# Who issues the loads that bring chunks of edge records back from DRAM: SyncE instead of GpSimd

## The chip, the cores and the metric

The kernel runs on one core of one Trainium2 chip. A core has engines with queues of their own: TensorE (PE in the profile; its weight loads are PEld), VectorE (DVE), ScalarE (ACT), GpSimd (POOL) and SyncE (SP). SyncE computes nothing: it issues DMA transfers. Each engine takes its instructions strictly in the order in which they stand, and an instruction that waits holds up all that stand behind it on its engine. The metric is device microseconds (us) of one execution.

## What is computed

The reference is one layer of a graph network, followed by a mixture of experts; what matters here is its edge part:

```
x  : 3125 nodes x 512        src, dst : 50000 edges, sorted by the dst that was drawn
out = segment_sum(edge_feat(x[src], x[dst], edge_attr), edge_dst)   # edge_dst = src array
x   = x + gnn(layernorm(x)) + linear_attention(layernorm(x))
x   = x + moe(layernorm(x))                                          # 8 experts, 2 per node
```

Every edge needs a record (its attributes through a small softplus layer, the two node numbers, a place). The sums go to the node that the edge points at, so the kernel first sorts the records by that node, in DRAM.

## The kernel before

It has three stages, one after the other.

**Stage 1** makes the records, sorts them and does all work by nodes. The 392 tiles of 128 edges are 14 chunks of CT = 28 tiles. For chunk c, `records(c)` (line 239) computes places (`at_i`, lines 210 to 232, VectorE) and records (`rec`), and stores them with one transfer of 672 KB, in the order of arrival, to the DRAM tensor `lined` (line 273, SyncE). `recall(c)` (line 382) brings such a chunk back to SBUF, to the tile `again`, of which there are two. `place` (line 387) then writes the chunk's 28 tiles one by one to their places in the DRAM tensor `recs`, with an indirect DMA each (line 395, GpSimd): 392 scatters. A chunk can be recalled when its store has landed, and when all 28 scatters of the chunk two before it have landed, since they read the buffer that it takes.

The node work beside it comes in three parts. `layer_norm(t)` (line 327) runs for 25 tiles of 128 nodes: it loads x (line 333, SyncE), normalizes, stores a first share of the output (line 353, SyncE), transposes, and ends with matmuls into `ps_kx` (line 364). Then come the products of the query features for 7 groups of nodes and 2 halves (line 535, `ps_nm`). Last, for 25 tiles again, the rows that the edges will gather are computed: the last matmul of a tile is line 620, the result lies in a tile `r` of which there are two (lines 600, 608, 609), and SyncE stores it to `rows_d` and `rows_s` (lines 610, 611), loads y (line 554) and stores y (line 626). A tile's `r` can be written again when both stores of the tile two before it have landed.

Some scatters are held back on purpose: `place(upto, behind)` hangs the first scatter of a group on a matmul ("POOL gives way to PE"), one on each of the 25 layer norms, on each of the 14 query products and on each of tiles 0 to 23 of the last part. A scheduler with costs of its own sets the order on every engine in stage 1. It puts a scatter that is held back behind others that are not, so the last scatter of a chunk stands on GpSimd among those of the next.

**Stage 2** (`run_pairs`, line 905) is written out by hand: SyncE fetches sorted records (line 699), GpSimd gathers rows (lines 710, 714), and 212 pairs of tiles pass through all engines. The first fetch waits for all 392 scatters. **Stage 3** (`run`, line 1242) is the mixture of experts.

Of the kernel before, what the change touches and what calls it, by code (L numbers as in the profile page):

```python
# [43 lines left out]
def gnn_mix_moe_kernel(ctx: ExitStack, tc: tile.TileContext, a: dict, out: bass.AP):  # L44
# [5 lines left out]
    nc = tc.nc  # L50
# [41 lines left out]
    lined = dram.tile([T // CT, P, CT, REC], F32, name="lined")  # L92
# [30 lines left out]
    with ExitStack() as c1:  # L123
# [256 lines left out]
        again = {}  # L380

        def recall(c):
            if c < T // CT:
                again[c] = chk.tile([P, CT, REC], F32, name="again", bufs=2)
                nc.gpsimd.dma_start(again[c], lined[c])

        def place(upto, behind=None):

            for t in range(len(placed), min(T, max(0, int(upto / 1.3)))):
                c, i = divmod(t, CT)  # L390
                if t == 0:
                    recall(0)
                if i == CT // 2:
                    recall(c + 1)
                put = nc.gpsimd.indirect_dma_start(  # L395
                    out=recs[:, :], out_offset=bass.IndirectOffsetOnAxis(ap=at_i[:, t : t + 1], axis=0),
                    in_=again[c][:, i, :], in_offset=None,
                )
                if behind is not None:
                    tc.add_manual_dep(  # L400
                        put.ins, behind.ins.name,
                        mybir.DependencyInfo(mybir.DependencyClass.Sync, mybir.DependencyReason.DATA),
                        reason="POOL gives way to PE",
                    )
                    behind = None
                placed.append(put)
# [998 lines left out]
```

## Time and profile before

| | |
|---|---|
| three runs | 2907.07, 2907.54 (median), 2909.65 us |
| the profiled execution | 2907.43 us, of which the span from first to last instruction 2905.7 us |
| mean granted TensorE clock | 0.942 |
| busy: PE, DVE, ACT, POOL | 86%, 64%, 50%, 61% |
| transfers of `lined` and `again` | 14 of 672 KB each |
| stage 1 | 0 to 658.6 us (the first fetch of stage 2) |

The profile's page gives busy time by engine, a picture of the span in 40 slices (72.6 us each), the DMA queues, the chain that ended last, and the costliest groups of instructions. The trace behind it can be asked for one tile's instructions, or for all instructions of a stretch in order of time; such a line has the start, the duration, the engine, the line of the code, the operation with output and input, the number of merged instructions and, in brackets, how long the engine was idle before and what ended it. SPq and POOLq are the sequencers that issue transfers.

### The profile page before, as it was taken

The page shows a single profiled execution, that of the slowest core. Times are in us where ns is not written, and L with a number is a line of the kernel's source. Part 1 is how long each engine was busy: PE and PEld are TensorE (multiplying, and loading weights), DVE is VectorE, ACT ScalarE, POOL GpSimd, SP SyncE. Part 2 cuts the span into 40 slices and gives each one's busy share as a digit, 9 for nine tenths or more (in the row PEclk, how much of TensorE's full clock was granted, in tenths as well). Part 3 has the DMA queues.
Part 4 walks back from the last instruction along what each step waited for, and adds up shares of the span by engine and source line. Part 5 has one row for each costly group of instructions (what it writes and reads, how often), then busy time and mean ns, then how long its engine had stood idle before and what let it go on. Part 6 is the DMA issues. An engine that isn't in the chain of part 4 may idle for free. (4 is left out here: it accounts for less than half of the span.)

```text
span 2905.7 us, 41979 instructions
## 1 busy us (share of the span) xinstructions
PE 2508.4 (86%) x13530; PEld 1631.8 (56%) x13530; DVE 1865.2 (64%) x3864; ACT 1463.4 (50%) x4183; POOL 1762.2 (61%) x1756
## 2 busy tenths in 40 slices
PE   2685999005999999999999999997499999999998
PEld 2463466003444444444444444444388888888887
DVE  5887322005999999999999999996722222222222
ACT  2472422003888888888888888884311111111111
POOL 1777766677766666666666666750255555555553
PEclk8897999556999999999999999999799999999999
DMA  6662066107888888888888887853642622975452
GB/s 261 205 221 86 27 234 217 44 27 236 268 258 258 259 257 258 255 262 257 258 258 257 259 258 251 256 181 116 252 150 72 226 87 71 323 276 200 168 189 98
DMA packets 191644, 588.10 MB, mean 202 GB/s; under 512 B 54405, under 2 KB 79418, under 8 KB 179384
## 3 DMA queue, kind: packets, MB, share of 16 engines
q0 software_dynamic: 135216, 496.50, 52.4%
q1 hardware_dynamic: 49864, 82.54, 8.5%
q10 hardware_dynamic: 6336, 6.28, 0.7%
q8 instruction: 111, 1.82, 0.2%
q14 instruction: 117, 0.96, 0.1%
HBM read 635.54 MB, written 119.53 MB: 260 GB/s over the span
## 5 line engine op out<-in xcount | busy, mean ns | idle before, releaser
L884 PE MATMUL ps_s<-ft,one 128*128 128x512 f32 x1696 | 765.3, 594 | 2.1 <-DVE ft L871 2.0
L710 POOL DMA_INDIRECT gd<-rows_d,rec x424 | 429.7, 1013 | 266.0 <-DVE h L758 158.2
L714 POOL DMA_INDIRECT gx<-rows_s,rec x424 | 434.9, 1026 | 129.2 <-issue 123.4
L395 POOL DMA_INDIRECT recs<-again,at_i x392 | 413.7, 1055 | 156.2 <-issue 122.1
L867 ACT ACTIVATE ft<-ft,rec 128x128 f32<-128x128 f32 x1272 | 395.3, 389 | 193.8 <-DVE ft L860 193.7
L884 PEld LDWEIGHTS ps_s<-ft,one 128*128 128x128 f32 x1696 | 312.2, 194 | 310.7 <-issue 231.2
L1280 ACT ACTIVATE h<-ps_f,bias 128x128 f32<-128x128 f32 x318 | 116.7, 367 | 620.8 <-PE ps_f L1267 617.0
L1267 PE MATMUL ps_f<-h,we 128*128 128x128 f32 x3392 | 401.3, 277 | 0.0
L1282 DVE TENSOR_SCALAR h<-ps_f,bias 128x128 f32<-128x128 f32 x318 | 111.4, 351 | 433.4 <-PE ps_f L1267 429.4
L1267 PEld LDWEIGHTS ps_f<-h,we 128*128 128x128 f32 x3392 | 386.9, 192 | 1.4
L1194 POOL DMA_INDIRECT we<-w_rows,w_at x212 | 215.1, 1014 | 222.2 <-PE ps_y L1298 98.0
L734 PE MATMUL ps_ip<-ident,prod 128*128 128x128 f32 x1272 | 165.9, 281 | 172.1 <-DVE prod L726 172.1
L734 PEld LDWEIGHTS ps_ip<-ident,prod 128*128 128x128 f32 x1272 | 140.3, 143 | 252.1 <-issue 249.3
L822 ACT ACTIVATE dot<-gx,rec 128x128 f32<-128x128 f32 x848 | 270.6, 397 | 0.0
L812 DVE TENSOR_TENSOR wt<-wt,wb 128x1024 f32<-128x1024 f32 x212 | 257.7, 1216 | 0.0
L805 PE MATMUL wb<-w_s,hT 32*128 32x512 f32 x848 | 240.8, 644 | 2.9 <-DVE wt L812 2.9
L801 PE MATMUL wa<-w_f,hT 32*128 32x512 f32 x848 | 240.0, 642 | 0.0
L726 DVE TENSOR_TENSOR prod<-gd,gx 128x768 f32<-128x768 f32 x212 | 201.9, 952 | 23.1 <-DMA gx<-rows_s,rec 23.1
L1267 PEld LDWEIGHTS ps_f<-xt,we 128*128 128x128 f32 x1696 | 199.4, 193 | 26.0 <-issue 23.4
L871 DVE TENSOR_TENSOR ft<-gx,wt 128x768 f32<-128x768 f32 x212 | 205.7, 970 | 0.0
L1267 PE MATMUL ps_f<-xt,we 128*128 128x128 f32 x1696 | 199.8, 277 | 0.7 <-ACT xt L1215 0.7
L1298 PE MATMUL ps_y<-we,h 128*128 128x512 f32 x424 | 196.1, 605 | 0.0
(303 smaller groups left out, 3755.6 us busy)
## 6 DMA issues: line engine op xcount, KB each, us to landing
w_rows<-in_Wh POOLq DMA_DIRECT2D x24, 1024.0 KB
rows_s<-r SPq DMA_DIRECT2D x24, 448.0 KB
recs<-zero POOLq DMA_DIRECT2D x10, 1056.0 KB
rec<-recs SPq DMA_DIRECT2D x106, 96.0 KB
lined<-rec SPq DMA_DIRECT2D x14, 672.0 KB
again<-lined POOLq DMA_DIRECT2D x14, 672.0 KB
w_rows<-in_Wo POOLq DMA_DIRECT2D x8, 1024.0 KB
gd<-rows_d,rec POOLq DMA_INDIRECT x424
```

The lines of the kernel that those rows point to most:

```text
L395: put = nc.gpsimd.indirect_dma_start(out=recs[:, :], out_offset=bass.IndirectOffsetOnAxis(ap=at_i[:, t : t + 1], axis=0), in_=again[c][:, ...
L710: nc.gpsimd.indirect_dma_start(out=Q.gd[:, (i + 2) % G, :], out_offset=None, in_=rows_d[:, :], in_offset=bass.IndirectOffsetOnAxis(ap=reci ...
L714: Q.last = nc.gpsimd.indirect_dma_start(out=Q.gx[:, i, :], out_offset=None, in_=rows_s[:, :], in_offset=bass.IndirectOffsetOnAxis(ap=reci[ ...
L734: nc.tensor.matmul(ps[:, i, :], Q.prod[:, i, b * P : (b + 1) * P], ident, is_transpose=True, start=(b == 0), stop=(b == 2),)
L801: nc.tensor.matmul(wa[:, k, :], Q.hT[r, 0, :], w_f2[r, :], start=True, stop=True)
L805: nc.tensor.matmul(wb[:, k, :], Q.hT[r, 1, :], w_s2[r, :], start=True, stop=True)
L812: nc.vector.tensor_mul(R.wt, R.wt, wb)
L822: nc.scalar.activation(R.dot[:, c - 1, k, :], x[:, i, c * MUL : (c + 1) * MUL], AF.Copy, scale=Q.rec[:, i, c : c + 1])
L867: nc.scalar.activation(R.ft[:, k, D + c * MUL : D + (c + 1) * MUL], R.ft[:, k, 2 * D :], AF.Copy, scale=Q.rec[:, i, c : c + 1],)
L884: nc.tensor.matmul(R.ps, R.one[:, k, :], R.ft[:, k, m * D : (m + 1) * D], start=(k == 0 and m == 0), stop=(k == 1 and m == 1),)
L1194: nc.gpsimd.indirect_dma_start(out=dst, out_offset=None, in_=src, in_offset=bass.IndirectOffsetOnAxis(ap=at[:, j : j + 1], axis=0), bounds ...
L1267: nc.tensor.matmul(pss[f], ws[l][:, k, f * P : (f + 1) * P], h[:, k, :], start=(k == 0), stop=(k == 3))
```

## The change

The transfer that brings a chunk back is issued by SyncE instead of GpSimd:

```diff
         def recall(c):
             if c < T // CT:
                 again[c] = chk.tile([P, CT, REC], F32, name="again", bufs=2)
-                nc.gpsimd.dma_start(again[c], lined[c])
+                nc.sync.dma_start(again[c], lined[c])
```

Bytes, buffers and what waits for what stay the same; the waits of the 14 transfers now stand in SyncE's queue, between its loads and stores. The scheduler also orders stage 1 anew: on PE, DVE and ACT the lines of `records`, `layer_norm` and `by_random` change places among each other, on GpSimd some scatters do. Stages 2 and 3 keep their order.

## The prediction

> **What bounds the kernel now.** I read first the page's picture in 40 slices, for the stage that the change touches, then the answer for the tile `again`, then instructions in order of time on POOL, SP and PE.
>
> ```profile
> PE   2685999005999999999999999997499999999998
> POOL 1777766677766666666666666750255555555553
> ```
>
> Slices 8 and 9 (508 to 653 us): PE has nothing to do, POOL works on. Stage 1 ends with the scatters.
>
> ```profile
> L395 POOL DMA_INDIRECT recs<-again,at_i x392: 952/958/14968, 67.3 to 656.3; - x196
> L385 POOL DMA_DIRECT2D again<-lined x14: 542/579/593, 52.9 to 612.3; - x14
>   DVE acc L684: 149.5, 1
> ```
>
> In the rows the durations are min/median/max in ns. Scatters are issued from 67.3 to 656.3 us, and the first write of stage 2's sums (L684) waits 149.5 us. PE's last matmul of stage 1 ends at 510.8, so the node work had about 146 us to spare against the scatters' end.
>
> What a scatter and a recall cost POOL is seen late in the stage:
>
> ```profile
> 568.03 0.96 POOL L395 DMA_INDIRECT recs<-again,at_i  x1 [0.30 <-issue]
> 570.46 0.58 POOL L385 DMA_DIRECT2D again<-lined  x1 [1.47 <-DMA recs<-again,at_i]
> 575.39 0.98 POOL L395 DMA_INDIRECT recs<-again,at_i  x1 [4.35 <-DMA again<-lined]
> 576.68 0.95 POOL L395 DMA_INDIRECT recs<-again,at_i  x1 [0.31 <-issue]
> ```
>
> A scatter takes 0.96 + 0.30 = 1.26 us. The recall waits 1.47 us until the scatter before it has landed, and the scatter behind it starts 4.93 us after the recall's start, when the chunk has landed. Nearly every recall is such a turn: the two buffers and the held-back scatters make the chain (last scatter of a chunk, landing, recall, landing, next chunk). Its length does not hang on who issues.
>
> **The change, part by part.** I count scatters by their place on POOL, from 0, and recalls by their chunk. The order of the built programs gives, for both, which scatter is the last of chunk c-2 and which the first of chunk c.
>
> *What goes from POOL.* Recall 2 stood between free scatters:
>
> ```profile
> 126.47 0.96 POOL L395 DMA_INDIRECT recs<-again,at_i  x1 [0.30 <-issue]
> 127.43 0.58 POOL L385 DMA_DIRECT2D again<-lined  x1
> 128.32 1.16 POOL L395 DMA_INDIRECT recs<-again,at_i  x1 [0.30 <-issue]
> ```
>
> 128.32 - 126.47 is 1.85, less 1.26: 0.6 us gained, and 0.6 again at recall 3. Recall 4 cost 209.43 - 205.57 - 1.26 = 2.6.
>
> *The turns.* New length, from the start of a chunk's last scatter to the first that reads the recalled chunk: 0.96 + 1.47 to the landing, then 0.3 (SP's transfers show 0.3 to 0.6 on its sequencer) and 4.5 to the recall's landing, sum 7.2 us. No transfer of this size with free engines is seen on SP. Bounds: 3.1 (96 KB, issued on SP at 658.63, gather at 661.69) and 9.2 (`lined` of chunk 1, issued at 53.18 beside weight loads; the wait ended at 62.39). I take POOL's row, 4.93, as the same bytes move. Each us more or less here is 1 us per turn. Before, the turns took, for recalls 5 to 13: 8.2, 7.8, 9.1, 9.5, 8.3, 10.8, 7.9, 7.4, 10.2. Against 7.2 they shorten by 1.0, 0.6, 1.9, 2.3, 1.1, 3.6, 0.7, 0.2 and 3.0 us. Recall 4 is a new turn: in the new order the last scatter of chunk 2 stands straight before the first of chunk 4 (before, ten were between): 7.2 - 1.3 = 5.9 lost. Running sum: 0.6 + 0.6 + 2.6 - 5.9 = -2.1 after recall 4; +9.1 before recall 12; +12.3 at the end. POOL alone would start its last scatter at 656.3 - 12.3 = 644.0.
>
> *What comes to SP.* Recalls 3 to 13 stand in its queue ahead of loads and stores, and wait for POOL. SP is free again at "start before, less the running sum, plus 2.7" (0.96 + 1.47 + 0.3). One scatter of 14.97 us (at 251.7, beside VectorE's L450 to L452, straight after the layer norms) moves with these, so I leave out 14 us from there to recall 7. SP is free of recalls 3 to 13 at 148, 220, 265, 307, 365, 404, 440, 483, 522, 562, 603.
>
> Behind recall 3 stand the x loads of layer norms 7 and 8:
>
> ```profile
> 118.58 0.33 SPq L273 DMA_DIRECT2D lined<-rec  x1
> 119.00 0.38 SPq L333 DMA_DIRECT2D x<-in_x  x1
> ```
>
> 119.0 becomes 149. Recall 4 holds layer norms 13 to 16, recall 5 norms 17 to 22, recall 6 the last two: x at 311 instead of 221.5. Norm 17 ended 20 us after its x was issued, norm 24 (253) 31 us after; so the last one now ends at 331 to 342, the first `ps_nm` (300) comes 47 us later at 378 to 389, tiles 0 and 1 (364) another 64 later at 442 to 453. All this, and the new order on PE, DVE and ACT, is hidden by the 146 us above. The issue itself, 14 times 0.33 us, is nothing on SP, which mostly waits.
>
> Then SP stands at recalls 7 to 10 until 483, and only then stores tiles 0 and 1; tiles 2 and 3 need their `r`. Behind recall 11 stand the stores of tiles 4 to 7, behind recall 12 (562) those of 8 to 14, behind recall 13 (603) from 15. So the spare time is used up, and the last leg is from recall 12 on. Its pattern is in the trace: two tiles' stores, then two more tiles, then the next group:
>
> ```profile
> 367.02 0.32 SPq L611 DMA_DIRECT2D rows_s<-r  x1
> ...
> 372.95 0.51 ACT L600 COPY r<-ps_p 128x416 f32<-128x416 f32 x1 [4.17 <-DMA rows_s<-r]
> ```
>
> Tile 0's `rows_s` (367.02) lets tile 2's copy start 5.9 us later, and tile 4's last matmul ends at 389.05: 22.0. With 1.2 from SP's release to `rows_s` of tile 8, tile 12 ends at 562 + 23 = 585. From tile 12 (440.04) to tile 24 (510.79) 70.8 us pass: 656. Recall 13 delays only the store of tile 15, which tile 17 needs 10 us later. The first fetch stands behind tile 24's stores on SP, the last issued 0.8 us after the last matmul; with one landing (2.5) it comes at 657 to 659. Before it came at 658.6.
>
> *PE's clock.* The granted clock was 0.50 from 260 to 280, while PE stood nearly idle, 0.55 from 280 to 285 and 1.00 after. In the new waits PE falls idle for 10 us and more, and pays such a start, at most 2.5 us (5 at half speed), on the last leg once: I take 1.5. The Trainium skill (TensorE: Matmul & The Clock Gate, Part 1) puts the warm-up at about 3.4 us at half clock; by that it would be 1.7.
>
> **The sum.** First fetch at 658 + 1.5 to 660, against 658.6: +0.5. Each release sends a burst (recall, two tiles' stores, a y: 2.3 MB, 9 us at the 261 GB/s seen from 365 to 402); a recall (364.75) was under way in the pattern's 5.9 us too, so I add only 1. Stages 2 and 3 keep their order and shift as a whole. 2907.4 + 1.5 is **2909 us**; the profiled execution is 0.1 below the median, so nothing is corrected. Own range 2901 to 2917: 4 from nine turns at 0.5, 4 from the leg.
>
> The Trainium skill (DMA: Bandwidth & Descriptors, Issuing engines are not separate DMA queues) says that all issuers share the same transfer engines and another issuer saves only its time to issue. By that alone 14 recalls at 0.6 us save 8. But the same page (Anatomy of one DMA) says that a wait is kept on the issuing sequencer: that speaks against the change, and here SP has most behind it.
>
> **The rivals.** I call 0.2% (5.8 us) about what a measurement can tell from no change.
>
> 1. *POOL stays the bound, and wins.* If the node work ends before 644, the fetch comes at 644.0 + 2.3 = 646.3: -12.3, or **2895 us**; with turns that gain only half of that, 2901. For it: 2 of the 22 us of the pattern were spent on matmuls which PE can do during the wait. Against it: 70.8 us of matmuls behind tile 12, at a clock already at 1.00. It decides from recall 12 at 549 or earlier, or a shorter leg.
>
> 2. *The ring of waits bites: slower.* POOL waits for SP's recall, SP for POOL's scatter, and scatters hang on matmuls whose x or `r` lie behind SP. Scatter 219 (401 us) hangs on the first `ps_nm` (378 to 389): 12 us to spare or more; scatter 330 (559) on tile 7, by the same pattern (tile 3's last matmul ended at 376.7) at 522 + 1.2 + 9.7 = 533: 26; scatter 358 (600) on tile 12 (585): 15. If the tiles behind a release take 10 us longer than the pattern, the last leg is 10 longer: 2919. From 15 on the scatters wait too: with 25, scatter 358 is 10 late, and the leg makes it **2934**; with more, recall 12 itself comes late, and the excess counts twice, up to 2950. For it: bursts, cold PE, a scheduler that does not know POOL's real pace. Against it: the pattern's row already holds a burst.
>
> 3. *Nothing moves*: the scheduler's order alone, with recalls harmless. 2907; only if SP never waits, which the order of 7 to 10 in a row excludes.
>
> **Chances.** Forecast 0.56 (faster 0.08, same 0.33, slower 0.15); rival 1 0.18, nearly all faster; rival 2 0.24, slower; rival 3 0.02. Together: faster 0.25, same 0.36, slower 0.39. The range leaves out little below and 0.1 of rival 2, from its own point on: 2895 to 2934.
>
> **What would show it.** No L385 on POOL, 14 on SPq; SP idle at L385 for 29 us before recall 3 and longer at recalls 8 to 10; layer norm 24 at 331 to 342; PE with short gaps up to 656 instead of empty slices 8 and 9; last scatter at 644 to 653, held by L620. Wrong it is if PE's last matmul of stage 1 comes before 645 (rival 1), or scatters wait for L364, L535 or L620 for 10 us and more before recall 12 (rival 2).

## The result, and the profile after

The changed kernel takes 2921.5 us (median of five, 2918.3 to 2927.2) against 2907.6 for the kernel before (median of five): ratio 1.0049, 95% interval 1.0033 to 1.0064, so 14 us slower. The forecast was 2909 and the range 2895 to 2934: the range holds it, "no change" does not. The profiled execution took 2926.8 us with a span of 2925.0, 5.3 us above the median, and all places in time below are from it.

The picture in slices and the answer for the tile `again`, after:

```profile
PE   2545595693999999999999999997589999999998
POOL 1776766665766666666766666650255555555553
```

```profile
L395 POOL DMA_INDIRECT recs<-again,at_i x392: 952/958/14626, 68.0 to 653.8; - x196
L385 SPq DMA_DIRECT2D again<-lined x14: 319/326/339, 52.1 to 607.7; - x14
...
  DMA again<-lined: 48.9, 9
  PE ps_own L620: 5.0, 3
```

PE's empty slices 8 and 9 are gone, PE works up to the end of stage 1, and scatters wait for the landing of a recall (48.9 us, 9 times) and, at the end, for L620. GpSimd is done 2.6 us earlier than before. But the first fetch of stage 2 comes not at 658.6 but at 673.4. The end of stage 1 before, with GpSimd's last scatter, SP's first fetch and GpSimd's first gather:

```profile
656.32 0.96 POOL L395 DMA_INDIRECT recs<-again,at_i  x1 [0.30 <-issue]
661.69 0.99 POOL L710 DMA_INDIRECT gd<-rows_d,rec  x1 [4.41 <-DMA rec<-recs]
```

```profile
658.63 1.76 SPq L699 DMA_DIRECT2D rec<-recs  x4
```

The same after, with PE's last matmul and SP's queue:

```profile
653.76 0.95 POOL L395 DMA_INDIRECT recs<-again,at_i  x1 [3.44 <-PE ps_own L620]
678.99 0.99 POOL L710 DMA_INDIRECT gd<-rows_d,rec  x1 [24.28 <-DMA rec<-recs]
```

```profile
659.45 0.60 PE L620 MATMUL ps_own<-w_ndo,xg 128*53 128x128 f32 x4
```

```profile
659.34 0.24 SPq L610 DMA_DIRECT2D rows_d<-r  x1
660.52 0.23 SPq L611 DMA_DIRECT2D rows_s<-r  x1
660.84 0.44 SPq L626 DMA_DIRECT2D out<-y  x1
673.37 5.47 SPq L699 DMA_DIRECT2D rec<-recs  x6
```

What SP waited for, from 655 to 690 us, and the state of the engines in two stretches of that wait (after the stretch and its length come the busy us of PE, PEld, DVE, ACT and POOL, with the number of instructions; the last three columns are PE's granted clock, the DMA engines' share, and GB/s):

```profile
SPq L699 <- DMA rows_s<-r: 11.8, 1, 11.8
```

```profile
664.00:668.00 4.00, 0.00 (x0) 0.00 (x0) 4.00 (x1) 0.00 (x0) 0.00 (x0) 0.58 0.15 36
668.00:672.00 4.00, 0.00 (x0) 0.00 (x0) 4.00 (x1) 0.00 (x0) 0.00 (x0) 0.50 0.07 25
```

The last scatter was issued at 653.8 and PE's last matmul ended at 660.0. The fetch waits 11.8 us for the store of tile 24's `rows_s`, issued at 660.52, and over most of that time the DMA engines are hardly used: 0.07 is about one of sixteen. Tile 24 has 53 rows. The trace's single packets show them one behind another: the 53 of `rows_d` from 660.09 to 664.93, the 53 of `rows_s` from 664.96 to 672.93, those of `out` from 672.96 to 677.20. The last of these still run while the first fetch does, which lands after 5.6 us (gather at 678.99) where it took 3.1 before.

So 14.7 us are lost up to the fetch, 2.6 in its landing, and the rest of the profiled 19.3 between there and the end; the last 2 of it appear between stage 2's last matmul (+17.8) and stage 3's first normalization (+19.5), which no run explains.

### The profile page after: what moved, and what is told of

Read it like the earlier page. It is cut to its first block, busy times and chain, and to the rows that moved or that the text cites. A ratio compares the mean times of both kernels' runs of the same rounds, so it can differ in the third digit from the quotient of the medians.

```text
span 2925.0 us, 42012 instructions
## 1 busy us (share of the span) xinstructions
PE 2528.2 (86%) x13530; PEld 1643.5 (56%) x13530; DVE 1865.7 (64%) x3864; ACT 1462.0 (50%) x4183; POOL 1755.3 (60%) x1742
```

## The experiments

The theory after the result: (1) the node work has become the bound, and its end is set by recall 12 alone, behind which SP holds tile 8's stores; (2) the last tile's three stores run row by row, a tail of 13 us that lay beside scatters before. Its rival: the loss is a little at every recall, collected over the ring of waits. The first four kernels ran on one chip, on which the kernel before took 2911.0 us (29 runs).

### The last tile's stores in two pieces

```diff
+                parts = [(0, n)] if n == P else [(0, 48), (48, n)]
-                nc.sync.dma_start(rows_d[rows, :], r[:n, : HID + 3 * MUL])
+                for a0, a1 in parts:
+                    nc.sync.dma_start(rows_d[t * P + a0 : t * P + a1, :], r[a0:a1, : HID + 3 * MUL])
...
```

(`rows_s` and `out` likewise; on the changed kernel, and as a control on the kernel before.)

> The changed kernel, with the three stores of the last tile (53 rows) each split in two, 48 rows and 5. Theory (the tail): in the changed kernel the first fetch waits 12.8 us from the issue of tile 24's rows_s (660.52) to 673.37, because the 53 rows of that store go one after another (the DMA share in that stretch is 0.06, one of 16 engines). 48 rows should spread: landing about 3 us after issue, first fetch at 664 to 665 instead of 673.4, and the first gather another 2 to 3 us earlier because no tile-24 store is left beside the fetch: 9 to 11 us off, so 2910 to 2913 by the median of 2921.5. Rival 1 (the store is late because ACT's small weight loads or the burst share its way): no change, 2921. Rival 2 (the whole loss is the ring of waits, the landing would have been hidden): no change, 2921.

> The kernel before (recalls on GpSimd), with the same split of the last tile's stores. Every theory of a tail: those stores land about 135 us before the last scatter, so nothing is on the path; 2907.6, within 3 us. If the split itself changes the program elsewhere, this run shows by how much.

Measured: 1.0007 (0.9998 to 1.0017) with recalls on SP, 2912.6 us, as expected, against 1.0049 without the split. SP's queue of the split kernel:

```profile
660.60 0.69 SPq L612 DMA_DIRECT2D rows_d<-r  x2
661.78 1.15 SPq L614 DMA_DIRECT2D rows_s<-r  x2
663.68 0.93 SPq L630 DMA_DIRECT2D out<-y  x2
665.29 2.88 SPq L703 DMA_DIRECT2D rec<-recs  x6
```

The same 53 packets of `rows_s` now lie between 662.58 and 663.94, 1.4 us instead of 8.0. PE's last matmul ends 1.3 us later than in the changed kernel (661.3), yet the first gather comes at 668.4 instead of 679.0: from last matmul to first gather 7.1 us instead of 18.9, so 11.8 us went there. Both rivals that expected no change fall. The control gave 0.9983 (0.9971 to 0.9994), a little below what was expected; its profile is ahead by 1.8 us at recall 6 already (317.8 against 319.6), long before the split stores, so the split is not shown to be the reason.

### Recalls 0 to 11 on SP, or only 12 and 13

```diff
-                nc.sync.dma_start(again[c], lined[c])
+                (nc.sync if c < 12 else nc.gpsimd).dma_start(again[c], lined[c])
```

(and the same with `c >= 12`.)

> Recalls 0 to 11 on SP, 12 and 13 on GpSimd. Theory (last leg): the release that counts is then recall 11 (525.5): tile 8 at 549 as in the changed kernel, then 94.4 us of node work to tile 24 (70.8 / 12 tiles x 16) gives 643, tail 13.3: 656; POOL's own last scatter comes at about 650 to 653, first fetch 656 to 657 instead of 673.4: 2904 to 2908. Rival (lateness that collects over all recalls, a share for each): two of eleven waiting recalls fewer, 2.5 us off the 14: 2919.

> Only recalls 12 and 13 on SP, 0 to 11 on GpSimd as before. Theory (last leg): recall 12 has the same place in SP's order (behind tile 7's stores, ahead of tile 8's) and waits for the same scatter, which comes up to 4 us later than in the changed kernel (570 instead of 566): tile 24 at 660 to 664, first fetch 673 to 677: 2921 to 2926, the whole loss from two recalls. Rival (lateness that collects over all recalls): 2908 to 2911.

Measured: 1.0055 (1.0039 to 1.0070), 2926.2 us, with only the last two on SP. Two recalls of fourteen make the whole loss. SP's queue in that kernel:

```profile
407.90 0.32 SPq L610 DMA_DIRECT2D rows_d<-r  x1
409.10 0.72 SPq L611 DMA_DIRECT2D rows_s<-r  x1
411.65 0.33 SPq L554 DMA_DIRECT2D y<-out  x1
...
568.23 0.32 SPq L385 DMA_DIRECT2D again<-lined  x1
568.65 0.38 SPq L554 DMA_DIRECT2D y<-out  x1
569.13 0.37 SPq L610 DMA_DIRECT2D rows_d<-r  x1
```

Tile 7's rows are stored at 409, as early as one would like. Then SP stands at recall 12 for 156 us, and tile 8's rows follow it at 569. Tile 24 ends at 661.0 and the fetch comes at 674.3, both as expected. The rival of collected lateness (2908 to 2911) falls.

With recalls 0 to 11 on SP the ratio is 1.0006 (0.9995 to 1.0018). The node work then ended at 647.8 (643 was expected) and was not the bound, as the theory says. But GpSimd's last scatter came at 661.8, not 650 to 653, and the fetch at 666.3; the 2912.4 us lie between the 2904 to 2908 expected and the rival's 2919. The largest part of that lateness stands at recall 13:

```profile
609.35 0.96 POOL L395 DMA_INDIRECT recs<-again,at_i  x1 [0.30 <-issue]
614.88 0.59 POOL L385 DMA_DIRECT2D again<-lined  x1 [4.57 <-DMA out<-y]
615.77 0.98 POOL L395 DMA_INDIRECT recs<-again,at_i  x1 [0.30 <-PE ps_own L620]
622.67 0.96 POOL L395 DMA_INDIRECT recs<-again,at_i  x1 [5.92 <-DVE xg L576]
```

```profile
610.00:615.00 5.00, 5.00 (x33) 3.80 (x33) 0.98 (x2) 0.99 (x2) 0.43 (x2) 1.00 0.88 314
```

The turn took 13.3 us where the kernel before needed 7.7. Both waits in it are longer: from the last scatter's start to the recall 5.5 us instead of 2.8, from the recall to the first scatter behind it 7.8 instead of 4.95. The node work, which in the kernel before had long ended there, keeps the DMA engines at 314 GB/s beside it (87 before). (The releasers named in the brackets are not what a recall or this scatter waits for; what ended last there are the landings.) So what the earlier release gives is taken back; that the traffic is the cause is not shown by a run of its own, but in the kernel before, too, the turns of recalls 7 to 10, beside the node work's 176 to 261 GB/s, took 9.1 to 10.8 us, and those of recalls 12 and 13 behind it 7.4 and 7.7.

### Taking the held-back scatters away, and a third buffer

These two pairs, and the four kernels after them, ran on two other chips, on which the kernel before itself took 3087.5 and 3054.9 us. Ratios are to it on the same chip, but in all these profiles the node work ends stage 1, whoever issues the recalls, so they do not repeat the case of the first chip.

```diff
-                if behind is not None:
+                if behind is not None and False:
```

> Recalls on GpSimd; the edge that holds one scatter per tile back behind a matmul is taken out (it serves the order alone), and the last tile's stores are split as in the run before. Now 29 scatters lie between the one a recall waits for and the first that needs it (1 to 3 before), so no recall should be a turn. Of the 589 us from first to last scatter, 392 x 1.263 = 495 are scatters, 59 the ten turns of recalls 4 to 13, the rest recalls and stretched scatters: last scatter at 600 to 605, first fetch 603 to 608 instead of 658.6, 2850 to 2858. The node work must end before that, as it did (511). If turns were not the cost of GpSimd's chain: 2900 or more.

> The same with recalls on SP. Theory (what stands behind a waiting recall): in SP's order recalls 11, 12 and 13 now stand one behind the other ahead of the first node store, and recall 13 waits for scatter 335, at 505 to 525. Tile 4 ends 22 later, tile 24 another 118 (20 x 5.9) later, the split store lands 4 later: first fetch 649 to 669, 2898 to 2918: 45 to 65 us slower than the same kernel with recalls on GpSimd. Rival (the ring through the two buffers is the whole cost, and with it open the engine that issues hardly matters): within 8 us of the GpSimd version, 2846 to 2858.

Measured: 1.055 (1.049 to 1.061) on GpSimd, 1.041 (1.038 to 1.045) on SP. Both expectations fall, also in their order. In the GpSimd version the scatters still end at 660.4 (recalls now wait for records), and the node work at 943.1. Two stretches of it (columns as above):

```profile
220.00:250.00 30.00, 22.40 (x83) 14.57 (x84) 26.39 (x88) 14.24 (x29) 13.39 (x13) 0.79 0.61 199
...
280.00:310.00 30.00, 0.00 (x0) 0.00 (x0) 2.66 (x11) 2.11 (x3) 22.99 (x25) 0.50 0.12 32
```

```profile
313.39 1.22 PE L360 MATMUL ps_k<-r_W_kT,xT 128*128 128x256 f32 x2 [37.45 <-issue]
```

Where GpSimd issues scatters without a break, the trace shows no matmul for 37 us and almost nothing on VectorE and ScalarE, with the DMA engines at 0.12; where GpSimd pauses, all work. So the held-back scatters are no mere burden here: beside the three-buffer kernel with recalls on GpSimd below, which ran on the same chip with them, GpSimd's scatters end 76 us earlier (660.4 against 736.8) and the node work 200 us later (943.1 against 743.1). What stops those engines is not shown and stays open, and so does whether the chip or the missing waits make it, as these two kernels ran on no other chip.

The third buffer (`again` with `bufs=3`, y tiles with four instead of five to make room, last tile's stores split):

> Recalls on GpSimd, three buffers instead of two (the y tiles have four instead of five, to make the room), last tile's stores split, scatters held back as before. Recalls 4 to 7 are no turns any more (10 scatters or more between), 8 to 13 still are (1 to 5 between): 5.0 + 5.7 + 5.3 + 6.5 = 22 us off: first fetch about 637, 2886; with the turns that are left a little shorter, 2880.

> The same with recalls on SP. Theory: in SP's order recall 11 now stands ahead of the first node store, 12 ahead of tile 4's and 13 ahead of tile 8's (with two buffers it was 12), and 13 waits for scatter 353, at about 580. Tile 12 ends 23 later at 603, tile 24 71 later at 674, first fetch 678: 2925 to 2932, though a buffer was added; some 40 to 45 us slower than the same with GpSimd. Rival (a third buffer opens the ring for both): 2880 to 2890 like its GpSimd twin.

Measured: 0.9963 (0.9946 to 0.9980) and 1.0034 (1.0002 to 1.0066). With GpSimd that is 13 us, not the 22 or more expected. SP is slower than GpSimd by 24 us of the medians, against 40 to 45 expected, and not level with it as the rival had it. But the place is another: the first `ps_nm` comes at 458.6 instead of 431.9, and the fetch at 776.7 instead of 748.8. The 27 us are there before the last part of the node work begins. That would fit x loads and other transfers of the layer norms and the records behind waiting recalls, but no run separates these.

### The node work's transfers on ScalarE's queue

```diff
-                nc.sync.dma_start(ys[t][: tn(t)], out[t * P : t * P + tn(t), :])
+                nc.scalar.dma_start(ys[t][: tn(t)], out[t * P : t * P + tn(t), :])
...
```

(and the stores of `rows_d`, `rows_s` and `out` in the same way; with the split.)

> Recalls on SP, and the node work's own transfers (y loads, the stores of rows_d, rows_s and out) moved from SP to ACT's queue, last tile's stores split. Nothing of the node work stands behind a recall any more, only the x loads of the layer norms do. Theory (the loss is what stands behind the waiting recalls on SP): tiles 0 and 1 at about 450 as in the changed kernel, tile 24 some 147 us later (364 to 511 before), at 600: hidden again. Then GpSimd's chain decides, 4 to 7 us shorter than before: last scatter at about 650, first fetch 652 instead of 658.6; ratio to the kernel before 0.997 to 0.999. Rival (a recall from SP is dear in itself, or its landing is): as the split run with recalls on SP, 1.0007 or more.

> Control: recalls on GpSimd, the node work's transfers on ACT, last tile's stores split. The node work has 130 us to spare, so nothing is on the path: like the split run with recalls on GpSimd, 0.998 to 1.000. The difference to the run before it is then what the recall's engine is worth once nothing stands behind it: 4 to 7 us for SP by the theory (0.0015 to 0.0025), 0 by the rival that GpSimd's chain does not hang on the issuer.

> Recalls on SP, the node work's transfers on ACT, three buffers, split. On top of the two-buffer version turns 4, 5 and 6 go (6.6 + 5.7 + 5.6 = 18 us net of the scatters in them): first fetch about 634, ratio 0.991 to 0.993. Rival (the third buffer moves the turns elsewhere, or the node work becomes the bound): 0.996 to 1.000.

> Three buffers, recalls on GpSimd, split, on the same chip as the run before it (the first time it ran beside a kernel before of 3087 us, 0.9963). Turns 4 to 7 go, 22 us: 0.9925 where the kernel before takes about 2910; with the other chip's stretched stage 1 0.996. If SP is worth 4 to 7 us once nothing stands behind it, this one is that much slower than the run before it.

Measured: recalls on SP 1.0020 (0.9995 to 1.0046), on GpSimd 0.9929 (0.9905 to 0.9953); three buffers with recalls on SP 1.0037 (1.0009 to 1.0066), on GpSimd without the move to ScalarE 0.9978 (0.9954 to 1.0003). I had expected SP ahead by 4 to 7 us once no node store stands behind a recall; it is 23 us behind, and 1.0020 is what the rival had (1.0007 or more). The premise was wrong there: the node work is the bound on this chip even with recalls on GpSimd (last matmul at 740.4, 757.0 with SP), so whatever still stands behind the early recalls, x loads among it, can cost directly; 14 of the 17 us between the two are there at the first `ps_nm` (427.6 instead of 413.5). That fits, but it does not rule the rival out on these chips. Whether the move to ScalarE would have hidden the waits on the first chip was not tried. The third buffer gave nothing there to the kernel with recalls on SP, where 0.991 to 0.993 was expected, and its gain with recalls on GpSimd (0.9963) is not clear of noise in the repeat (0.9978).

The fastest against the kernel before is the one with GpSimd's recalls, the node work's transfers on ScalarE and the split: 0.9929. As the kernel before was not profiled on that chip, why it gains is not shown.

## Why the prediction was right and where it failed

| step | predicted | measured (profiled execution) |
|---|---|---|
| SP free of recalls 3, 5, 8, 10 | 148, 265, 404, 483 | issued at 147.5, 261.9, 405.1, 486.6 |
| SP free of recalls 12, 13 | 562, 603 | 566.2, 607.7 |
| last layer norm, first `ps_nm`, tiles 0 and 1 | 331 to 342, 378 to 389, 442 to 453 | 341.4, 386.8, 453.0 |
| recall 12 to tile 12, tile 12 to 24 | 23, 70.8 | 23.1, 70.8 |
| clock restart, burst | 1.5, 1 | nothing beyond the pattern |
| tile 24's last matmul to the first fetch | 0.8 + 2.5 | 13.3 |
| turn, new length | 7.2 | 6.9 to 8.2, median 7.6 |
| GpSimd's lead after recall 12 | 9 | 4.0 (scatter 331 at 571.40, before 575.39) |

**The leg.** That recall 12 sets the end, that recall 13 costs nothing, that the early recalls are hidden, and the length of the leg came out as worked out, and the two runs that split the recalls show it from both sides. SP's queue at recall 12, after:

```profile
542.04 0.44 SPq L626 DMA_DIRECT2D out<-y  x1
566.23 0.32 SPq L385 DMA_DIRECT2D again<-lined  x1
566.64 0.38 SPq L554 DMA_DIRECT2D y<-out  x1
567.12 0.38 SPq L610 DMA_DIRECT2D rows_d<-r  x1
```

Tile 8's `rows_d` follows the recall, after SP has stood for 24 us. That recall 12 and not 13 does it is read from this trace, where the 70.8 us behind tile 12 are those of the kernel before; no run moved recall 12 alone.

**The failed step: "with one landing (2.5)".** That term of the sum measured 12.8 (from 660.52 to 673.37). I took the landing of a small transfer for that of the last tile's store. The price stood in the trace that I had: in the kernel before, the same store is issued at 511.26 and its packets end at 524.19, 12.9 us, beside scatters that hid it:

```profile
511.26 0.23 SPq L611 DMA_DIRECT2D rows_s<-r  x1
```

The run with the split took the long landing away and 12 us of the loss with it. The Trainium skill (DMA: Bandwidth & Descriptors, Why a DMA increments its semaphore by 16 and not by 1) has a rule that I did not use: a transfer runs on the largest number of engines up to 16 that divides the outer sizes of both its sides. That gives one engine for 53 rows and sixteen for 48, and agrees with 0.07 of the DMA engines, 25 GB/s, and with 8.0 against 1.4 us.

**The mis-sized term: the turns.** GpSimd's chain was to win 9.1 us before recall 12; it won 4. Between a recall's issue on SP and the first scatter lie 5.3 us in the median where I had 4.8 (0.3 + 4.5). One turn after the change, first GpSimd's lines, then SP's:

```profile
563.96 0.96 POOL L395 DMA_INDIRECT recs<-again,at_i  x1 [0.30 <-issue]
571.40 0.97 POOL L395 DMA_INDIRECT recs<-again,at_i  x1 [6.48 <-DMA again<-lined]
```

```profile
566.23 0.32 SPq L385 DMA_DIRECT2D again<-lined  x1
```

The turn is 7.4 us, before it was 7.4 too. Counted as in the prediction, between the places that bound the turns in the new order, recalls 5 to 13 took 79.3 us before and take 68.3 now: 11.0 less where I had 14.4. (By the old order's own places it was 78.0.) About 5 us are missing from the lead before recall 12: 2.8 in the turns of recalls 5 to 11; 0.7 in that of recall 4, which took 7.8; 0.7 in the first scatter, which starts at 68.0 instead of 67.3; and 0.8 between the other scatters. So SP was released 4 us late at recall 12, and that went into the end at full price.

The sum itself was added up 1.7 us short: its own terms, 656 + 0.8 + 2.5 + 1.5 (clock) + 1 (burst), put the fetch at 661.8, 3.2 us after 658.6, not the 1.5 that went into 2909. With 4.2 more (recall 12), 10.0 more (tail) and 2.5 less (clock and burst, not seen) it comes to 673.5; the fetch came at 673.4.

**The rivals.** Rival 1 (GpSimd stays the bound, and wins) failed at its own point: recall 12 came at 566, not 549 or earlier. Rival 2 had the sign and the size, but not the mechanism: its condition, 10 us more from a release to the tiles behind it, did not occur, and scatters waited for L364, L535 or L620 for 0.6 us in all before recall 12, not for 10. I had put 0.39 on slower; the forecast's own range, 2901 to 2917, does not hold 2921.5 and was too narrow at the end of the leg, where a term of one line carried the result. What holds it is the part of the wide range that was put there for rival 2. That is luck: the loss is of another kind. Rival 3 (nothing moves) fell with the 14 us.

## What to carry to other kernels

When a change moves the end of a stage to other work, price the whole tail of that work anew, and read the landings of its last transfers in the trace even where they were hidden before. A wait put into a queue costs what stands behind it: here two of fourteen recalls, and by the trace one of them, made the loss, and moving the other twelve came out even. A last tile's store of 53 rows that ends a stage belonged in two transfers, of 48 and 5 rows.

## What was not expected of the hardware

- A store of 53 rows goes row by row: 53 packets of 3584 bytes in 8.0 us, against 1.4 us as 48 and 5 rows. With recalls 0 to 11 on SP, such a store of `out` (660.99 to 665.50) also stood beside the last scatter, and the fetch came 4.5 us after that scatter's issue, where it took 2.3 before.
- Without the held-back scatters, on the chip where the kernel before takes 3087 us, PE, VectorE and ScalarE nearly stand still for 20 to 37 us at a time while scatters are issued without a break. In the kernel before, on the first chip, PE was busy for 97 of the 100 us from 300 to 400, beside 69 us of GpSimd's work. The cause is open.
- The scatter of 15 us moved with VectorE's L450 to L452, as the prediction assumed (14.6 us at 339.8).
